# The latents' second normalization taken from the first one's scale and variance, and the order of the opening, in a two-layer cross-attention and mixture-of-experts kernel

## The chip, the cores and the metric

The kernel runs on one NeuronCore of one Trainium2 chip. The metric is the device time of one execution in microseconds (us), taken as a median over several executions: 2829.24 us for the kernel before, from three executions between 2828.84 and 2831.44. The profile is of a separate execution. Engine names are those of the profile: PE is TensorE's matrix multiplication and PEld its weight load, DVE is VectorE, ACT is ScalarE, POOL is GpSimd, SP is SyncE, which here issues most of the DMAs.

## The reference, cut to what matters

The input `x` holds 4 batches of 512 latents of 256 numbers; `ctx_1024` holds 4 batches of 1601 context rows of 256 numbers. Four layers follow one another, each added to `x`: a cross-attention with 8 heads of 128, an expert layer with two experts for each token, a second cross-attention, a second expert layer. The change touches the first cross-attention alone:

```
def _layernorm(x, axis=-1, eps=1e-05):            # outside the layer
    m, v = mean(x), var(x)
    return (x - m) / sqrt(v + eps)

def _L0_xattn_ref(x, latents, gamma_media, beta_media, gamma_lat, beta_lat, Wq, bq, Wkv, bkv, Wo, bo):
    xn = _layernorm(x, gamma_media, beta_media)         # the context
    ln = _layernorm(latents, gamma_lat, beta_lat)       # the latents
    q = ln @ Wq + bq
    kv_input = concatenate([xn, ln], axis=1)            # 1601 + 512 rows
    k, v = split(kv_input @ Wkv + bkv)
    out = softmax(q k^T / sqrt(128)) v                  # per head
    return out @ Wo + bo

x = x + _L0_xattn_ref(ctx_1024, _layernorm(x), ...)
```

The latents are normalized twice, one normalization straight after the other. The first has no gain and no shift, so its result has mean zero, and its variance follows from the variance `v` of `x`: with `s = 1/sqrt(v + eps)` it is `v * s * s`.

## The kernel before

**Stages.** The first cross-attention fills the span up to about 1575 us, the rest follows. For each of the four batches the normalized latents and context rows are turned (features on the partitions) into one tile `kvin`, which all eight heads read: the 512 latents stand in the first column group, the context rows behind them. A head takes its queries from the latents' columns of `kvin` (line 767), its keys from all columns (line 783, five pieces of which the first, `keys(0)`, covers 512 columns, the latents' among them), its values (line 817), then scores (line 834), row maximum on DVE (line 842), exponential on ACT (line 848), an exchange of blocks by DMA (line 855), a 32x32 block transpose on DVE (line 863), the weighted sum of values (line 871) and the output projection (line 882). The scores have one PSUM buffer of five banks (`a_ps_s`), so the next scores wait for the exponential of the last. All other PSUM results of this layer rotate through the two buffers of the pool `ps_t`.

**The normalization helpers.** `ln_moments` runs `bn_stats` and `bn_aggr` on DVE for each tile of 128 rows (lines 127 and 128) into `mv`, which holds mean and variance. `ln_scale` turns the variances of all tiles into scales: `ve = variance + eps` (line 137), a square root on ACT (line 144), a reciprocal on DVE (line 149) and one Newton step of four small DVE operations (lines 152 to 155). `ln_apply` subtracts the mean and multiplies by the scale (line 159), one DVE operation of 128x256 for each tile. `layernorm` is all three. A batch of latents has four tiles.

**`keys_input(b, ctx_b)`** makes the steps that fill `kvin` for one batch. `latents` normalizes `x[b]` into the tile `lat`; `latents_again` normalizes `lat` in place; `group` turns four tiles of 128 rows with PE transposes into two PSUM tiles `tp` (line 683), one for each half of the features, and writes each into `kvin` with gain and shift: the first half on DVE (line 708), the second on ACT (line 700). For batch 0, `first(n0)` takes the statistics of up to four context tiles on DVE (lines 725 and 726), their scale and a shift `away` (line 729), and applies both on ACT (line 733).

**The opening.** For batch 0 these steps are written in an order by hand, and `in_order(*computing)` keeps their instructions on PE, DVE, ACT and POOL in exactly that order (an instruction from elsewhere may stand between them):

```
latent, context = keys_input(0, ctx_b)     # latents, latents_again, group of the latents
*qk, fill = queries_keys(0)                # queries, keys(0) .. keys(4)
stats, turns = context[::2], context[1::2] # first(n0), ctx_group(n0)
for s in (latent[:2] + stats[:1] + latent[2:] + fill[:2] + stats[1:2] + turns[:1] + stats[2:3] + ...):
    s()
```

So the first context group's statistics stand ahead of the writing of the latents into `kvin`, on DVE and on ACT alike. The loads of the opening are issued by SP in an order of their own (`in_order(nc.sync)`, lines 629 to 648): `x` of batch 0, the first context group, the small vectors, the first head's parts of the weights, then the other context groups and weights.

**After the opening** the framework's scheduler sets the order on each engine from the order of the text and the dependencies; it may move an instruction ahead of others on its engine. For batches 1 to 3 the steps of `keys_input` are attached to the heads 5 to 7 of the batch before: `latents` and `latents_again` to one query tile each, `group` later. The tile `lat` has one buffer (pool `a_gone`), which between the opening and batch 1 is a scrap tile under the same tag. The Sqrt of line 144 and the Exp of line 848 need different tables on ACT; where one follows the other an `ACT_TABLE_LOAD` stands ahead of it.

Of the kernel before, what the change touches and what calls it, by code (L numbers as in the profile page):

```python
# [8 lines left out]
F32 = mybir.dt.float32  # L9
I32 = mybir.dt.int32  # L10
AF = mybir.ActivationFunctionType
ALU = mybir.AluOpType
# [4 lines left out]
P = 128  # L17
B, S, D = 4, 512, 256
M = 1601
NT = S // P  # L20
NX = B * NT
DC = D // P
EPS = 1e-5
# [51 lines left out]
def xattn_ffn_twice(ctx: ExitStack, tc: tile.TileContext, a: dict, out: bass.AP):  # L75
    nc = tc.nc
# [41 lines left out]
    def ln_moments(pool, src, n, tail=P, mv=None, some=None):  # L118

        if mv is None:  # L120
            mv = pool.tile([P, n, 2], F32, tag=f"mv{n}", name="mv")
            if tail < P:
                nc.vector.memset(mv, 1.0)
        for i in range(n) if some is None else some:
            r = rows_of(i, n, tail)
            st = pool.tile([P, 6], F32, tag="bnst", name="st")
            nc.vector.bn_stats(st[:r], src[:r, i, :])
            nc.vector.bn_aggr(mv[:r, i, :], st[:r])
        return mv

    def ln_stats(pool, src, n, tail=P):

        return ln_scale(pool, ln_moments(pool, src, n, tail), n)

    def ln_variance(pool, mv, n):
        ve = pool.tile([P, n], F32, tag=f"ve{n}", name="ve")
        nc.vector.tensor_scalar(ve, mv[:, :, 1], EPS, None, ALU.add)
        return ve

    def ln_root(pool, mv, n, ve=None):  # L140
        if ve is None:
            ve = ln_variance(pool, mv, n)
        rs = pool.tile([P, n], F32, tag=f"rs{n}", name="rs")
        nc.scalar.activation(rs, ve, AF.Sqrt)
        return ve, rs

    def ln_scale(pool, mv, n, root=None):
        ve, rs = root or ln_root(pool, mv, n)
        nc.vector.reciprocal(rs, rs)

        t = pool.tile([P, n], F32, tag=f"nt{n}", name="t")
        nc.vector.tensor_tensor(t, rs, rs, ALU.mult)
        nc.vector.tensor_tensor(t, t, ve, ALU.mult)
        nc.vector.tensor_scalar(t, t, -0.5, 1.5, ALU.mult, ALU.add)
        nc.vector.tensor_tensor(rs, rs, t, ALU.mult)
        return mv, rs

    def ln_apply(dst, src, mv, rs, i, r=P):
        nc.vector.tensor_scalar(
            dst[:r, i, :], src[:r, i, :], mv[:r, i, 0:1], rs[:r, i : i + 1], ALU.subtract, ALU.mult  # L160
        )

    def layernorm(pool, dst, src, n):
        mv, rs = ln_stats(pool, src, n)
        for i in range(n):
            ln_apply(dst, src, mv, rs, i)
# [10 lines left out]
    x = [const.tile([P, NT, D], F32, name=f"x{b}") for b in range(B)]  # L177
# [13 lines left out]
    def clear_slots(zeros, i):  # L191
# [24 lines left out]
        fill=0.0,  # L216
# [365 lines left out]
    with ExitStack() as st:  # L582

        w = st.enter_context(tc.tile_pool(name="a_w", bufs=1, side="right"))
        gone = st.enter_context(tc.tile_pool(name="a_gone", bufs=1, side="right"))
        rt = st.enter_context(tc.tile_pool(name="a_rt", bufs=1, side="right"))
        one = st.enter_context(tc.tile_pool(name="a_one", bufs=1))
        two = st.enter_context(tc.tile_pool(name="a_two", bufs=2))
# [61 lines left out]
        def add_output_bias(b):  # L650
            for i in range(NT):
                nc.gpsimd.tensor_tensor(x[b][:, i, :], x[b][:, i, :], bo, ALU.add)

        def keys_input(b, ctx_b):

            state = {}
# [5 lines left out]
                state["ctx"] = ln_scale(two, state["mv"], NM)  # L662

            def latents():
                state["lat"] = lat = gone.tile([P, NT, D], F32, tag="lat", name="lat")
                layernorm(two, lat, x[b], NT)

            def latents_again():
                layernorm(two, state["lat"], state["lat"], NT)
                if b:  # L670
                    add_output_bias(b)

# [64 lines left out]
            if b == 0:  # L737
                steps = [latents, latents_again, lambda: group(state["lat"], 0, NT, 0, gbl, P, NT)]
                return steps, [
                    f for n0 in range(0, NM, 4) for f in (lambda n0=n0: first(n0), lambda n0=n0: ctx_group(n0))  # L740
                ]
# [5 lines left out]
                lambda: moments(range(8, NM)),  # L747
                scale,
                latents,
                latents_again,  # L750
            ] + [lambda n0=n0: apply(n0) for n0 in range(0, NM, 4)]
            late = [lambda: group(state["lat"], 0, NT, 0, gbl, P, NT)]
# [157 lines left out]
        latent, context = keys_input(0, ctx_b)  # L910
        *qk, fill = queries_keys(0)

        stats, turns = context[::2], context[1::2]
        for s in (
            latent[:2] + stats[:1] + latent[2:] + fill[:2] + stats[1:2] + turns[:1] + stats[2:3]
            + turns[1:2] + fill[2:3] + stats[3:] + turns[2:3] + fill[3:4] + turns[3:] + fill[4:]
        ):
            s()
# [24 lines left out]
        for n in range(n_steps + 4):  # L943
            b, h, t = n // (H0 * NT), n // NT % H0, n % NT
# [143 lines left out]
    turns = soonst.enter_context(tc.tile_pool(name="turns", bufs=2))  # L1088
# [143 lines left out]
    with ExitStack() as st:  # L1232
        two = st.enter_context(tc.tile_pool(name="b_two", bufs=2, side="right"))
# [120 lines left out]
        again = nc.values_load(odds_i[0:1, 0:1], min_val=0, max_val=2 * E)  # L1354
# [65 lines left out]
    with ExitStack() as st:  # L1420
        one = st.enter_context(tc.tile_pool(name="c_one", bufs=1))
        two = st.enter_context(tc.tile_pool(name="c_two", bufs=2))
# [276 lines left out]
    with ExitStack() as st:  # L1699
        one = st.enter_context(tc.tile_pool(name="d_one", bufs=1))  # L1700
        two = st.enter_context(tc.tile_pool(name="d_two", bufs=2))
# [202 lines left out]
        state = {}  # L1904
# [46 lines left out]
        for k, long in enumerate(SURE):  # L1951
            i = sum(long == other for other in SURE[:k])
# [157 lines left out]
```

## Time and profile before

| | |
|---|---|
| time, median of three executions | 2829.24 us (2828.84 to 2831.44) |
| time of the profiled execution | 2828.22 us |
| its span on the core | 2826.2 us |
| mean granted TensorE clock | 0.986 |
| first scores' row maximum (line 842) starts | 51.16 us |
| first cross-attention ends, about | 1575 us |

The profiled execution's time is 2.0 us above its span, which is what lies around the span. In the rows that follow, a row of the timeline gives start, duration, engine, line, operation, output and inputs with their shapes, the number of merged instructions, and in brackets the idle time of the engine before it and what ended that idle time. A matrix product of float32 is recorded as two instructions, so `x4` for queries is two products, one for each half of the features.

### The profile page before, as it was taken

How to read it: one execution, taken by the hardware profiler on the slowest of the kernel's cores; microseconds unless marked ns; L12 is line 12 of the kernel's file. 1: busy time of each engine (PE TensorE's matmuls, PEld its weight loads, DVE VectorE, ACT ScalarE, POOL GpSimd, SP SyncE). 2: the span in 40 equal slices, each digit the busy share in tenths (PEclk: the TensorE clock that was granted, in tenths of full speed). 3: DMA queues.
4: the chain of work that ended last, by engine and by line, in shares of the span. 5: the costliest groups of instructions: out<-in, count | busy, mean ns of one | idle time of the engine just before them, and what ended most of it. 6: DMA issues, size and time to landing. Idle time of an engine off the chain costs nothing. (4 is left out here: it accounts for less than half of the span.)

```text
span 2826.2 us, 36019 instructions
## 1 busy us (share of the span) xinstructions
PE 2706.3 (96%) x13566; PEld 1851.0 (65%) x13566; DVE 1468.9 (52%) x2343; ACT 940.0 (33%) x1362; POOL 260.0 (9%) x292
## 2 busy tenths in 40 slices
PE   5999999999999999999999899998999898889998
PEld 2666666666766666766666687774455454458887
DVE  6544547544476444545444421137887878872111
ACT  3333334323233332333233211214444444442221
POOL 0000000100000000001000002001110201022542
PEclk9999999999999999999999999999999999999999
DMA  5444443433343344334334545535631111025573
GB/s 164 110 115 113 104 103 95 114 95 84 95 119 91 102 100 100 89 85 113 95 84 125 176 154 175 169 97 144 178 81 40 38 31 54 33 71 193 166 229 89
DMA packets 196435, 311.95 MB, mean 110 GB/s; under 512 B 43319, under 2 KB 117368, under 8 KB 193560
## 3 DMA queue, kind: packets, MB, share of 16 engines
q1 hardware_dynamic: 157512, 227.52, 29.4%
q0 software_dynamic: 14160, 46.31, 5.5%
q10 hardware_dynamic: 24576, 35.68, 4.9%
q8 instruction: 111, 1.82, 0.3%
q14 instruction: 76, 0.62, 0.1%
HBM read 111.73 MB, written 51.34 MB: 58 GB/s over the span
## 5 line engine op out<-in xcount | busy, mean ns | idle before, releaser
L842 DVE TENSOR_REDUCE top<-ps_s 128x1 f32<-128x2113 f32 x128 | 301.8, 2358 | 581.0 <-PE ps_s L834 581.0
L871 PE MATMUL ps_o<-pT,v 128*128 128x256 f32 x2176 | 521.6, 381 | 0.5 <-DVE inv L849 0.5
L834 PE MATMUL ps_s<-kT,qT 128*128 128x512 f32 (+1 forms) x1280 | 489.0, 526 | 5.8 <-ACT attn L848 5.8
L871 PEld LDWEIGHTS ps_o<-pT,v 128*128 128x128 f32 x2176 | 409.9, 191 | 115.1 <-issue 68.4
L848 ACT ACTIVATE attn<-ps_s,top 128x2113 f32<-128x2113 f32 x128 | 259.0, 2024 | 476.7 <-DVE top L842 452.0
L834 PEld LDWEIGHTS ps_s<-kT,qT 128*128 128x128 f32 x1280 | 241.6, 191 | 252.5 <-issue 236.6
L863 DVE STREAM_TRANSPOSE pT<-swapped 128x2176 f32<-128x2176 f32 x128 | 312.4, 2441 | 33.8 <-DMA swapped<-attn 23.7
L1195 DVE TENSOR_REDUCE tops<-ps_s 128x2 f32<-128x1024 f32 (+1 forms) x224 | 238.3, 1106 | 102.9 <-PE ps_s L1184 101.7
L783 PE MATMUL ps_k<-kvin,wkv 128*128 128x512 f32 (+1 forms) x640 | 263.6, 535 | 4.1 <-DVE mv_g L721 2.1
L1453 PE MATMUL ps_w<-asked,keyed 64*128 64x256 f32 (+1 forms) x1664 | 225.2, 405 | 35.1 <-DVE tops L1195 33.9
L817 PE MATMUL ps_v<-wkv,kvin 128*128 128x256 f32 x1088 | 254.5, 381 | 0.0
L1466 ACT ACTIVATE pT<-ps_w 128x1024 f32<-128x1024 f32 x192 | 189.8, 1022 | 150.7 <-PE ps_w L1453 139.4
L817 PEld LDWEIGHTS ps_v<-wkv,kvin 128*128 128x128 f32 x1088 | 204.8, 190 | 34.9 <-issue 4.5
L1453 PEld LDWEIGHTS ps_w<-asked,keyed 64*128 64x128 f32 (+1 forms) x1664 | 150.3, 188 | 110.2 <-DVE tops L1195 53.5
L1471 DVE TENSOR_TENSOR sum<-sum,pT 128x1024 f32<-128x1024 f32 x176 | 214.8, 1221 | 13.5 <-PE ps_o L1480 4.9
L796 ACT ACTIVATE kT<-ps_k,bqk 128x512 f32<-128x512 f32 (+1 forms) x160 | 96.9, 620 | 265.9 <-PE ps_k L783 130.5
L783 PEld LDWEIGHTS ps_k<-kvin,wkv 128*128 128x128 f32 x640 | 116.2, 192 | 78.6 <-issue 68.0
L824 ACT COPY v<-ps_v 128x512 f32<-128x512 f32 x144 | 79.9, 561 | 215.9 <-PE ps_v L817 143.9
L1184 PE MATMUL ps_s<-kv,qT 32*128 32x512 f32 (+1 forms) x1024 | 134.7, 553 | 9.3 <-DVE tops L1195 5.1
L1269 PE MATMUL ps_h<-sxT,w 128*128 128x256 f32 x512 | 116.1, 384 | 3.7 <-ACT hT L1276 3.7
L1283 PE MATMUL ps_y<-w,hT 128*128 128x256 f32 x512 | 115.1, 380 | 0.0
L1269 PEld LDWEIGHTS ps_h<-sxT,w 128*128 128x128 f32 x512 | 97.9, 192 | 20.5 <-ACT hT L1276 4.5
(302 smaller groups left out, 2525.2 us busy)
## 6 DMA issues: line engine op xcount, KB each, us to landing
swapped<-attn SPq DMA_DIRECT2D x1536, 68.0 KB, 2.0
swapped<-attn ACTq DMA_DIRECT2D x512, 68.0 KB, 2.2
w<-in_w_dram SPq DMA_DIRECT2D x32, 1024.0 KB, 6.0
rows_b<-empty SPq DMA_DIRECT2D x36, 530.0 KB, 4.4
w_e<-in_wall_dram SPq DMA_DIRECT2D x5, 2052.0 KB
cw<-in_ctxT_dram SPq DMA_DIRECT2D x4, 1601.0 KB
keyed<-kv SPq DMA_DIRECT2D x32, 200.1 KB, 3.6
ctx_b<-in_ctx_dram SPq DMA_DIRECT2D x3, 1536.0 KB
```

The source lines that it names most:

```text
L783: nc.tensor.matmul(ps[:, :n], lhsT=wkv[:, c, hs], rhs=kvin[:, c, : NB - 1, k, :] if k < 4 else kvin[:, c, NB - 1, :, :], start=c == 0, sto ...
L817: nc.tensor.matmul(ps[:, k, :], lhsT=flat_kvin[c][:, j * P : (j + 1) * P], rhs=wkv[:, c, cols], start=c == 0, stop=c == DC - 1,)
L834: nc.tensor.matmul(flat[:, j0 : j0 + n], lhsT=qT[:, t * P : (t + 1) * P], rhs=kT[:, j0 : j0 + n], start=True, stop=True,)
L842: nc.vector.tensor_reduce(top, flat[:, :L], AX.X, ALU.max, negate=True)
L848: nc.scalar.activation(attn[:, :L], flat[:, :L], AF.Exp, bias=top, accum_out=total)
L863: nc.vector.transpose(pT[:, :, k * P : (k + 1) * P].rearrange("p c (a i) -> p a c i", a=4), swapped.rearrange("p a (c i) -> p a c i", i=32),)
L871: nc.tensor.matmul(ps, lhsT=v[:, j - parts[part][0], (h % 2) * DH0 : (h % 2 + 1) * DH0], rhs=pT[:, j, :], start=j == 0, stop=j == NB - 1,)
L1195: nc.vector.tensor_reduce(tops[u][:, t : t + at // n, 2 * pair : 2 * pair + 2, j0 // 512], of, AX.X, ALU.max,)
L1269: nc.tensor.matmul(ps[:, f, :], lhsT=w1[:, c, (f0 + f) * P : (f0 + f + 1) * P], rhs=sxT[:, c, :], start=c == 0, stop=c == DC - 1,)
L1453: nc.tensor.matmul(ps[:r, s, pair * QH : (pair + 1) * QH], lhsT=keyed[o][64 * s : 64 * s + 64, pair, j * P : j * P + r], rhs=asked[u % 3][ ...
L1466: nc.scalar.activation(pT[:r], ps[:r], AF.Exp)
L1471: nc.vector.tensor_tensor(sums[u, 0], sums[u, 0], pT, ALU.add)
```

## The change

The step `latents` keeps only statistics and scale of `x[b]`. The step `latents_again` computes the second scale from the first scale and the variance, multiplies the two scales, and applies mean and product to `x[b]` at once. The opening's list of steps has the latents' `group` directly behind `latents_again`, ahead of `first(0)`.

```
             def latents():
+                state["once"] = ln_stats(two, x[b], NT)
+
+            def latents_again():
+                mv, once = state["once"]
+                ve = two.tile([P, NT], F32, tag="again", name="ve_a")
+                nc.vector.tensor_tensor(ve, once, once, ALU.mult)
+                nc.vector.tensor_tensor(ve, ve, mv[:, :, 1], ALU.mult)
+                nc.vector.tensor_scalar(ve, ve, EPS, None, ALU.add)
+                _, rs = ln_scale(two, mv, NT, ln_root(two, mv, NT, ve))
+                nc.vector.tensor_tensor(rs, rs, once, ALU.mult)
                 state["lat"] = lat = gone.tile([P, NT, D], F32, tag="lat", name="lat")
-                layernorm(two, lat, x[b], NT)
-
-            def latents_again():
-                layernorm(two, state["lat"], state["lat"], NT)
+                for i in range(NT):
+                    ln_apply(lat, x[b], mv, rs, i)
                 if b:
                     add_output_bias(b)
...
         for s in (
-            latent[:2] + stats[:1] + latent[2:] + fill[:2] + stats[1:2] + turns[:1] + stats[2:3]
+            latent + stats[:1] + fill[:2] + stats[1:2] + turns[:1] + stats[2:3]
             + turns[1:2] + fill[2:3] + stats[3:] + turns[2:3] + fill[3:4] + turns[3:] + fill[4:]
         ):
```

For a batch this takes away four `bn_stats`, four `bn_aggr`, one addition of eps and four applications on DVE, and adds four operations of 128x4 (the three that make `ve_a` and the product of the scales). The square root on ACT and the five operations behind it stay. Batches 1 to 3 run the same two steps; nothing else in the list of their steps is changed.

## The prediction, made before the changed kernel was run

> **What bounds the kernel now.** I read the engines' shares first, then busy time by stretch, then PE's waits, then the opening's timeline. The chain of waits on the page covers only the last 25 us and doesn't bear on this change.
>
> ```profile
> PE 2706.3 (96%) x13566; PEld 1851.0 (65%) x13566; DVE 1468.9 (52%) x2343; ACT 940.0 (33%) x1362; POOL 260.0 (9%) x292
> ```
> ```profile
> 24.40:50.00 25.60, 18.83 (x55) 8.70 (x55) 12.06 (x49) 11.51 (x25) 0.00 (x0) 0.87 0.37 110
> 50.00:78.40 28.40, 24.28 (x72) 12.83 (x70) 23.38 (x68) 16.61 (x20) 0.00 (x0) 0.94 0.38 96
> 78.40:1552.00 1473.60, 1473.10 (x5517) 1000.72 (x5518) 755.37 (x915) 476.32 (x655) 44.34 (x52) 1.00 0.40 101
> ```
> ```profile
> PE ps_s L834 <- ACT attn L848: 0.6, 1, 0.6
> PE ps_p L882 <- ACT oT L1013: 0.5, 1, 0.5
> ```
>
> The stretches give length, then busy time of PE, PEld, DVE, ACT and POOL, the granted clock, DMA share and GB/s. From 78.4 to 1552 us PE is busy for 1473.10 of 1473.60 us at full clock, and the last two lines are all that PE waits for there: 1.1 us. Whatever DVE or ACT does less of in that stretch is worth nothing; a time saved before 78.4 passes through whole. Before it PE is not the bound, and the change's order is made there:
>
> ```profile
> 9.18 1.38 DVE L159 TENSOR_SCALAR lat<-x,mv,rs 128x256 f32<-128x256 f32 x4
> ...
> 10.48 0.42 DVE L127 BATCH_NORM_STATS2 st<-lat 128x6 f32<-128x256 f32 x1
> ...
> 12.73 0.17 DVE L137 TENSOR_SCALAR ve<-mv 128x4 f32<-128x4 f32 x1
> ...
> 14.19 1.38 DVE L159 TENSOR_SCALAR lat<-lat,mv,rs 128x256 f32<-128x256 f32 x4
> ...
> 14.75 2.20 PE L683 MATMUL tp<-ident,lat 128*128 128x128 f32 x8 [14.75 <-DVE lat L159]
> 15.48 0.42 DVE L725 BATCH_NORM_STATS2 st<-ctx_b 128x6 f32<-128x256 f32 x1
> ...
> 19.40 0.81 DVE L708 TENSOR_SCALAR kvin<-tp,gbl 128x512 f32<-128x512 f32 x1
> 19.51 2.07 ACT L733 ACTIVATE ctx_b<-ctx_b,away,rs 128x256 f32<-128x256 f32 x4 [1.23 <-DVE away L729]
> ...
> 20.31 4.07 PE L767 MATMUL ps_q<-kvin,wq 128*128 128x512 f32 x4 [3.36 <-issue]
> 21.49 0.76 ACT L700 ACTIVATE kvin<-tp,gbl 128x512 f32<-128x512 f32 x1
> ...
> 24.41 0.75 DVE L774 TENSOR_SCALAR qT<-ps_q,bqk 128x512 f32<-128x512 f32 x1 [4.21 <-PE ps_q L767]
> ...
> 25.08 0.42 DVE L725 BATCH_NORM_STATS2 st<-ctx_b 128x6 f32<-128x256 f32 x1
> ```
>
> The transposes of the latents are done at 16.95, but DVE copies their first half out at 19.40 only, behind the first context group's statistics, and ACT the second half at 21.49, behind four context tiles. So PE stands for 3.36 us, and DVE then stands for 4.21 us for the queries (24.41) before the second context group. From 25.08 to 35.4 DVE has no gap; the opening is DVE's.
>
> **The second normalization, batch 0.** Removed between 9.18 and 12.73: four applications (9.18 to 10.48, 1.30 us) and four pairs of statistics (10.48 to 12.73, 2.25 us). The rest, from `ve` at 12.73 to the application at 14.19, stays (1.46 us, with the root on ACT and 0.27 us of waiting for it). Added are four 128x4 operations; `ve` gets in place of one of them, so three are net. Such dependent operations start 0.20 us apart (8.58, 8.78, 8.98, 9.18): 0.60 us. Net 3.55 - 0.60 = **2.95 us**: the application starts at 11.24 and ends at 12.62, PE's transposes end at 14.0.
>
> **The moved copies.** DVE now waits for the first four transposes. They follow the last application (12.62) by about 0.5 us (before, 15.57 to about 16.1), so the copy runs at 13.2 to 14.0 and DVE stands 0.6 us that it didn't. Queued behind it are the context statistics, which start at 14.0 instead of 15.48 and need 3.99 us to the end of `away` (15.48 to 19.47): 18.0. ACT copies the second half at 14.0 to 14.8, then has nothing until the context's root. PE starts the queries 0.10 us after DVE's copy (20.21 to 20.31): 14.1, finds ACT's half ready at 16.1, and ends after 4.07 us at 18.2. `qT` starts at 18.2 instead of 24.41: **6.2 us**. The two chains (context on DVE 18.0, queries on PE 18.2) end together, so what is late next is both.
>
> Does the rest follow by 6.2? On ACT the context tiles of the first group are applied at 18.05 to 20.1, only 1.5 us earlier than before, but the next in line, `kT` of `keys(0)` (26.98), would come at 20.8: 0.7 us to spare. No DMA is moved on SP. The loads: x, three context groups and tail, the small vectors and first weight parts are about 2.44 MB in one queue, and the DMA view's 2-us slices add up to 2.2 MB by 12 us and 2.87 MB by 14 us. The second group is wanted at 18.9, the third at 23.6. The gains and shifts of the latents (0.002 MB behind 1.05 MB) are in by 8, as the gain vectors behind them land 1.7 us after their issue at 6.96. I take 6.2 for everything up to 78.4.
>
> **The clock.** Queries take 4.07 us for x4 at 20.31 and 1.88 at 100.48: the array starts at half speed. The Trainium skill (TensorE: Matmul & The Clock Gate, Part 1) says that a free-running window of about 3.4 us of sustained work lifts the gate and an idle one closes it, and (Part 4) that transposes don't count as work. Moving the queries right behind the transposes then wins no speed: they take 4.07, as in my sum. If transposes did count, queries could end near 16.0 and DVE's 18.0 would decide: 6.4 us. The rule that speaks against the change is the closing: the granted clock was 0.50 from 32.8 to 39.6, and that period can fall on other work. The row bounds it: matmuls of x4 took 3.75 there against 1.95 at 41.63. One such group more or less on the path is 1.8 us either way.
>
> **Batches 1 to 3.** DVE loses per batch about 3.5 us and gains 0.8; with 755 of 1474 us busy this hides beside PE. Cover gone, it would be 8 us over three batches. PE's, POOL's and SP's order comes out the same in the built kernel. One thing moves: the root of batch 1's second scale no longer hangs on an application into `lat`, whose buffer the scrap holds, so the scheduler pulls it from about 286 us to the values of the first heads (about 82), with its table load and the reload of Exp ahead of the exponential at 87.28. ACT has 1.67 and 2.44 us idle before the copies there; the first load (1.28) and the root (0.21) fit in, the reload delays that exponential by 1.28. The Trainium skill (ScalarE: Activation LUTs, What ACT_TABLE_LOAD costs) reckons 1283 ns and a drain of 1380 ns: 2.66 us. The rows show no drain (load at 289.60, 1.28; the one at 74.93 is followed by its exponential at 76.22). Either way the next scores stand at 95.53 on PE, and the exponential ended at 89.4: room for 6 us. I put it at nothing; the same pair leaves 286 us, where it was hidden too.
>
> **The sum.** 2826.2 - 6.2 = 2820.0 span, with 2.0 around it 2822.0 for a profiled run. That run was 1.0 under the median, so 2829.24 - 6.2 = **2823.0 us**, 0.22% faster. The measurement can tell about 0.2%, 5.7 us, from no change: the forecast lies just past it.
>
> **Rivals.**
> - **Part is given back in the opening** (0.38). The half-clock period falls on `keys(0)` (its four start 0.85 us apart at half speed and 0.45 at full, which two of them had: 0.8 us), whose `kT` stands ahead of the second group's root on ACT; or on the first scores (48.22, 2.91 for x8: up to 2.9 more). Or the context chain is the true bound and only DVE's 1.5 us count (2827.7). For it: ACT's applications move by 1.5 only. Against the last: DVE's 4.21 us of standing for queries is plain in the row. Gain 1.5 to 5.6, typically 4: 2825.
> - **Slower through the clock gate** (0.07). Place: 19 to 78 us, where the second row above has 24 of 28 us busy at 0.94. Work that comes sooner leaves gaps elsewhere; if the gate closed for eight more windows of 3.4 us, each costs half its length, 1.7: 13.6 - 6.2 = 7.4 slower, 2836.6. It decides from four windows on. Against it: the order of gaps behind `qT` is the same, only earlier.
> - **The hoisted root stalls PE**: if the reload came before 78.4, where PE waits on exponentials (0.65 at 78.39), it would cost its 1.3 to 2.8: 2825. The order has it behind the copies; counted within the first rival.
>
> **Numbers.** Forecast 0.55, partial gain 0.38, slower 0.07. The range joins the forecast's own (6.2 with 1.8 on either side: 2821 to 2825) with most of the partial gain, and a little luck with the clock: 2820.0 to 2827.0. Faster by over 0.2%: 0.55; within: 0.38; slower: 0.07.
>
> **What will show it.** Line 159 on `lat` at 11.2; DVE's copy into `kvin` at 13.2; queries on PE at 14.1; `qT` at 18.2; first row maximum at 44.9 instead of 51.16; PE's waits from 72 to 1546 still about 1 us. Wrong if `qT` comes later than 19, if DVE shows a gap between 19 and 29, or if the row maximum at 84.89 - 6.2 is followed by PE waiting for `attn`.

## The result and the profile after

The changed kernel takes 2821.28 us (median of ten executions, 2819.25 to 2825.64) against 2828.28 us of the kernel before on the same chip (ten, 2824.97 to 2832.88). The ratio is 0.9976 with a 95% interval from 0.9968 to 0.9985: faster by 0.15 to 0.32%, some 7 us. The prediction said 2823.0 and 6.2. In us the interval reaches from about 4 to 9, so the times alone confirm the size only roughly; the timeline does it more closely.

The opening, from the timeline of the changed kernel (start, duration, engine, line, operation; its lines behind the change stand ten higher than before):

```profile
11.22 1.38 DVE L159 TENSOR_SCALAR lat<-x,mv,rs 128x256 f32<-128x256 f32 x4
...
11.78 2.21 PE L693 MATMUL tp<-ident,lat 128*128 128x128 f32 x8 [11.78 <-DVE lat L159]
13.17 0.81 DVE L718 TENSOR_SCALAR kvin<-tp,gbl 128x512 f32<-128x512 f32 x1 [0.57 <-PE tp L693]
13.90 0.42 DVE L735 BATCH_NORM_STATS2 st<-ctx_b 128x6 f32<-128x256 f32 x1
14.02 0.78 ACT L710 ACTIVATE kvin<-tp,gbl 128x512 f32<-128x512 f32 x1 [4.04 <-PE tp L693]
...
14.04 3.39 PE L777 MATMUL ps_q<-kvin,wq 128*128 128x512 f32 x4
...
17.59 0.16 DVE L739 SCALAR_TENSOR_TENSOR away<-mv_g,rs 128x4 f32<-128x4 f32 x1
17.68 0.75 DVE L784 TENSOR_SCALAR qT<-ps_q,bqk 128x512 f32<-128x512 f32 x1
...
28.05 3.75 PE L793 MATMUL ps_k<-kvin,wkv 128*128 128x512 f32 x4 [2.12 <-DVE mv_g L731]
...
44.40 2.36 DVE L852 TENSOR_REDUCE top<-ps_s 128x1 f32<-128x2113 f32 x1 [6.94 <-PE ps_s L844]
```

The latents are applied 2.97 us earlier than before, DVE's copy into `kvin` starts at 13.17 instead of 19.40, and `qT` at 17.68 instead of 24.41. The idle time ahead of `qT`, 4.21 us before, is gone; in its place stands 0.57 us for the transposes. The 6.7 us last: the first row maximum starts at 44.40 instead of 51.16.

Then comes the stretch in which PE is the bound, by its summary and by PE's waits:

```profile
71.70:1546.00 1474.30, 1472.98 (x5516) 1000.29 (x5517) 747.20 (x884) 475.59 (x654) 44.35 (x52) 1.00 0.40 101
```
```profile
PE ps_v L827 <- ACT v L834: 1.3, 2, 0.8
PE ps_s L844 <- ACT attn L858: 0.6, 1, 0.6
```

DVE does 8 us less here (747.20 against 755.37) and PE is busy as long as before. PE's waits, all shown above, are 1.9 us instead of 1.1.

The profiled execution is the slowest of the ten (2825.64 us), and it shows more than the opening. The first weighted sum starts 6.7 us earlier than before (79.8, before 86.5), the first weighing in the second cross-attention 7.0 us (1911.1, before 1918.1), the last one there only 2.7 us (2520.9, before 2523.6). From these two profiles alone, one would have read a gain of 2.6 us; the ten executions say 7.

### The profile page after: what moved, and what is told of

Same layout as the page of the kernel before. It is cut to its first block, busy times and chain, and to the rows that moved or that the text cites. A ratio compares the mean times of both kernels' runs of the same rounds, so it can differ in the third digit from the quotient of the medians.

```text
span 2823.9 us, 35983 instructions
## 1 busy us (share of the span) xinstructions
PE 2711.7 (96%) x13566; PEld 1853.8 (66%) x13566; DVE 1458.4 (52%) x2307; ACT 939.3 (33%) x1362; POOL 262.4 (9%) x292
```

## The experiments

The kernels were timed in groups, each beside the kernel before on the same chip. In the last group the kernel before and the changed kernel both take some 8 us longer than in the first, so ratios are compared. A ratio is not the quotient of the two medians and can differ from it by some hundredths of a per cent.

| kernel | `qT` at, us | first row maximum, us | median, us | ratio to before, 95% interval |
|---|---|---|---|---|
| before | 24.41 | 51.16 | 2828.28 | 1 |
| changed kernel | 17.68 | 44.40 | 2821.28 | 0.9976 [0.9968, 0.9985] |
| norm_only | 21.47 | 49.60 | 2825.90 | 0.9991 [0.9984, 0.9998] |
| order_only | 20.58 | 47.29 | 2825.30 | 0.9982 [0.9973, 0.9992] |
| batch0_only | 17.74 | 45.95 | 2822.30 | 0.9976 [0.9964, 0.9988] |
| later_only | 24.08 | 50.86 | 2830.84 | 1.0003 [0.9992, 1.0013] |
| after_again | 17.57 | 45.52 | 2829.60 | 0.9976 [0.9966, 0.9985] |
| warm | 17.59 | 43.09 | 2823.09 | 0.9955 [0.9942, 0.9967] |
| tail_root | 17.39 | 43.45 | 2824.91 | 0.9959 [0.9946, 0.9972] |
| warm_tail | 17.57 | 42.16 | 2823.20 | 0.9954 [0.9941, 0.9967] |

In norm_only to later_only before had a median of 2829.05, in the last four 2835.86. The arrival of `x` differs by up to 0.4 us between profiles (first statistics at 5.17 in tail_root, at 5.53 in warm), and all that follows with it.

### The normalization alone

The changed kernel with the opening's old list:

```
-            latent + stats[:1] + fill[:2] + ...
+            latent[:2] + stats[:1] + latent[2:] + fill[:2] + ...
```

> The new normalization with the opening's old list (first context statistics ahead of the latents' copies into kvin). Theory (two separate gains in the opening, then PE-bound): only the 2.95 us of DVE work are gone, everything in the opening shifts by that; qT at 21.4 instead of 24.41, first row maximum at 48.2 (before 51.16, changed kernel 44.40), time about 3 us under before. Rival (the normalization is all that counts, the order only follows it): first row maximum near 44.5, about 7 us under before. Rival (the copies' place is all): 51.2, no difference.

From its timeline:

```profile
16.45 0.81 DVE L718 TENSOR_SCALAR kvin<-tp,gbl 128x512 f32<-128x512 f32 x1
...
21.47 0.75 DVE L784 TENSOR_SCALAR qT<-ps_q,bqk 128x512 f32<-128x512 f32 x1 [4.21 <-PE ps_q L777]
...
38.65 3.32 PE L793 MATMUL ps_k<-kvin,wkv 128*128 128x512 f32 x4 [1.64 <-DVE kvin L718]
```

The whole chain stands 2.95 us earlier with the same gaps in it, to the 4.21 us of standing for the queries. The row maximum, though, came 1.56 us and not 2.95 us earlier (49.60, expected 48.2). The missing 1.4 us lie on the last row: these keys took 3.32 us, in before 1.95 us (at 41.63). The granted clock was at half from 39.1 to 42.5 here, of which more below. The ratio, 0.9991, is 0.09% of the 0.24% that the whole change brings.

### The order alone

The old two normalizations with the new list (the same edit the other way, on the kernel before).

> The old two normalizations with the new list of the opening. Theory: DVE's copy starts 3.0 us later than in the changed kernel, at 16.1, context scale done and qT at about 20.6 (before 24.41), first row maximum at 47.4, time about 3.8 us under before; together with norm_only this adds up to the changed kernel's 6.8. Rival (DVE's added wait for PE gives the gain back): qT not before 23, row maximum at 50 or later.

```profile
16.08 0.81 DVE L708 TENSOR_SCALAR kvin<-tp,gbl 128x512 f32<-128x512 f32 x1 [0.57 <-PE tp L683]
...
20.58 0.75 DVE L774 TENSOR_SCALAR qT<-ps_q,bqk 128x512 f32<-128x512 f32 x1
```

`qT` is 3.83 us earlier than before, and DVE waits 0.57 us for the transposes, as in the changed kernel. The parts add up at this point: 2.94 + 3.83 = 6.77, measured together 6.73. So the larger part of the gain at `qT` is not in the saved arithmetic but in where the copies stand. The row maximum is 3.87 us earlier (47.29, expected 47.4). In the times each part alone is faster than before; the two add up to 0.27% beside the 0.24% of the whole, and their intervals overlap, so which part is larger is read from the timeline and not from the times.

### Batch 0 alone, and batches 1 to 3 alone

batch0_only keeps the old two normalizations for `b > 0` behind an `if`, with the new list; later_only has the old ones for `b == 0` and the old list.

> New list, new normalization in batch 0, the old two normalizations in batches 1 to 3. Theory (PE hides all of batches 1 to 3): first row maximum 44.4 and a time within 1 us of the changed kernel's; PE's waits between 72 and 1546 about 1 to 2 us as in both kernels. Rival (the DVE work saved in batches 1 to 3, or the root pulled forward to the first heads, shows in the time): 2 us or more beside the changed kernel, slower if the saved work counted, faster if the pulled root cost.

> Old list and old normalizations in batch 0, the new normalization in batches 1 to 3. Theory: first row maximum at 51.2 and a time within 1 us of before; PE does not wait for the exponential that the table load delays. Rival (pulled root stalls PE in the first heads): 1.3 to 2.8 us of new PE waits between 78 and 110 and as much more time.

The ratios are 0.9976, the changed kernel's, and 1.0003. Batches 1 to 3 bring and cost nothing that can be measured; the interval of later_only alone leaves room for some 2 us gained to 4 us lost, and PE's waits narrow it. The root that the scheduler pulled forward is in later_only too, with its two table loads (ACT's timeline):

```profile
81.88 1.28 ACT L144 ACT_TABLE_LOAD   x1
83.17 0.20 ACT L144 ACTIVATE rs<-ve_a 128x4 f32<-128x4 f32 x1
...
86.93 1.28 ACT L863 ACT_TABLE_LOAD   x1
88.23 2.02 ACT L863 ACTIVATE attn<-ps_s,top 128x2113 f32<-128x2113 f32 x1
```

The first load and the root end before the next copy is due (83.52), the second delays the exponential by its 1.3 us, and PE has no new wait for `attn`: 0.6 us in total from 71.7 to 1546, as in before. PE's waits for the copies `v`, none listed in before, are 1.2 us in later_only and 1.3 us in the changed kernel, but also 1.0 in order_only, which has the old normalizations everywhere; the new arithmetic isn't needed for them.

### The changed kernel again, and PE kept at work

Two profiles had now shown a first row maximum later than their `qT` let expect. In both, norm_only and batch0_only, the granted clock fell twice in the opening. The view by stretch of batch0_only (length, then busy PE, PEld, DVE, ACT, POOL, granted clock, DMA share, GB/s):

```profile
25.10:32.00 6.90, 5.01 (x11) 2.42 (x12) 2.97 (x15) 3.48 (x9) 0.00 (x0) 0.51 0.63 182
32.00:35.30 3.30, 1.39 (x9) 0.84 (x8) 1.91 (x8) 2.06 (x5) 0.00 (x0) 1.00 0.00 0
35.30:38.70 3.40, 3.13 (x5) 0.90 (x3) 0.23 (x1) 0.45 (x2) 0.00 (x0) 0.50 0.00 0
```

The second period lies on the keys of line 798; the first row is of batch0_only, the second of the changed kernel, whose profile has one period only:

```profile
34.92 3.40 PE L798 MATMUL ps_k<-kvin,wkv 128*128 128x512 f32 x4 [1.64 <-DVE kvin L723]
```
```profile
34.88 1.95 PE L793 MATMUL ps_k<-kvin,wkv 128*128 128x512 f32 x4 [1.18 <-DVE kvin L718]
```

That is the 1.5 us between the row maxima, 45.95 and 44.40. The next run repeats the changed kernel, and "warm" adds matmuls that nobody reads:

```
+        warming = ps_o.tile([P, 2 * P], F32, tag="o", name="ps_warm")
+        def warm(n):
+            for _ in range(n):
+                nc.tensor.matmul(warming[:, :P], lhsT=ident, rhs=before, start=True, stop=True)
...
+        warm(20)
-            ... + turns[:1] + stats[2:3] + turns[1:2] + fill[2:3] + ...
+            ... + turns[:1] + [lambda: warm(4)] + stats[2:3] + turns[1:2] + [lambda: warm(8)] + fill[2:3] + ...
```

> The changed kernel once more, beside the next three. Theory: qT at 17.7 and, with one half-clock period of 6.8 us around 27 to 34, the first row maximum at 44.4; with a second period in the opening, as two other runs had, about 1.5 us later. Time about 6.8 us under before in the mean.

> The changed kernel with matmuls on PE whose result nobody reads: 20 of 128x128 ahead of the opening, 4 behind the first context group, 8 behind the second, in PE's gaps. Theory (the half-clock period lies on the path between 28 and 34, the queries' half clock does not, since qT stands behind the context scale): qT stays at 17.7, no half-clock period before 50, keys of line 793 at 28 no longer take 3.75 us, first row maximum at about 43.5 (0.9 less). Rival (the fill is in the way, or DVE alone sets the opening): 44.4 or later.

The changed kernel repeated gave the same ratio, 0.9976, and this time two separated periods of 3.4 us at half clock in the opening, with the row maximum at 45.52. In "warm" the opening's clock by stretch and PE's timeline:

```profile
14.40:17.80 3.40, 3.40 (x5) 1.33 (x4) 2.82 (x15) 0.30 (x2) 0.00 (x0) 0.50 0.93 326
20.00:27.00 7.00, 5.45 (x35) 3.87 (x35) 5.81 (x27) 3.80 (x10) 0.00 (x0) 1.00 1.08 357
27.00:34.00 7.00, 4.39 (x19) 2.25 (x18) 3.41 (x14) 5.16 (x11) 0.00 (x0) 1.00 0.37 101
```
```profile
2.12 7.31 PE L927 MATMUL ps_warm<-before,ident 128*128 128x128 f32 x40 [2.12 <-POOL before L212]
11.74 1.74 PE L693 MATMUL tp<-ident,lat 128*128 128x128 f32 x8 [2.31 <-DVE lat L159]
13.95 3.37 PE L777 MATMUL ps_q<-kvin,wq 128*128 128x512 f32 x4 [0.47 <-DVE kvin L718]
...
27.96 1.10 PE L793 MATMUL ps_k<-kvin,wkv 128*128 128x512 f32 x2 [0.33 <-DVE mv_g L731]
29.36 1.13 PE L793 MATMUL ps_k<-kvin,wkv 128*128 128x512 f32 x2 [0.30 <-ACT kvin L710]
```

From 20 to 34 the clock is full, and the keys at 28 are done by 30.5 instead of 31.8. The row maximum is 1.31 us earlier than in the changed kernel's first profile (0.9 expected) and 2.43 us earlier than in the repeated one. "No half-clock period before 50" was wrong for one: PE stood for 2.31 us at 9.4, and the clock fell at 14.4 (in warm_tail, below, too). The queries took 3.37 us in it, and `qT` stayed at 17.59: the queries' clock is not on the path here.

### The last context group's root moved forward

On ACT the root of the last context group stood behind a copy `kT` that waits for PE's keys, and DVE stood 3.99 us for it in the changed kernel, as in before. The edit moves its statistics and root ahead of those keys' copy:

```
-            + turns[1:2] + fill[2:3] + stats[3:] + turns[2:3] + ...
+            + turns[1:2] + stats[3:] + fill[2:3] + turns[2:3] + ...
```

> The changed kernel with the last context group's statistics and root written ahead of keys(1), so that on ACT the root no longer stands behind the copy kT that waits for PE. Theory: the 3.99 us that DVE stands for this root go, what is late next are PE's transposes of the third group at half clock; row maximum at 43.2 (1.2 less). Rival (PE's keys are the bound there anyway): 44.4.

> Both together. Theory: transposes of the third group end near 31.6, DVE copies them at 31.4 instead of 33.7, first row maximum at about 42.1, time about 2.3 us under the changed kernel's. Rival: no more than the better of the two.

DVE's waits between 26 and 45 us, first in the changed kernel, then in tail_root (in total, times, longest):

```profile
...
DVE rs L149 <- ACT rs L144: 4.3, 2, 4.0
DVE kvin L718 <- PE tp L693: 2.2, 1, 2.2
```
```profile
...
DVE kvin L718 <- PE tp L693: 4.0, 2, 2.6
DVE rs L149 <- ACT rs L144: 1.5, 1, 1.5
```

DVE's wait for ACT falls from 4.3 to 1.5 us, and a wait for PE's transposes, 1.8 us more, takes part of its place. The row maximum is 0.95 us earlier, of which 0.29 belong to an earlier `x` (DVE's first copy at 12.88 instead of 13.17); 0.66 remain of the 1.2 expected, as the second half of the transposes (33.52) now waits for DVE's copy. With both edits it is at 42.16, 2.24 us under the changed kernel's first profile, as expected, though the transposes of the third group did not end near 31.6: their second half, from 32.24, waits for DVE's copy here too. In the times, warm, tail_root and warm_tail have ratios of 0.9955, 0.9959 and 0.9954, each with an upper end of 0.9972 or less, against 0.9976 [0.9966, 0.9985] for the changed kernel beside them. All three beat the kernel before and stand under the changed kernel by 0.17 to 0.22%, with intervals that still overlap; which of the three is best, five executions each don't tell. These 5 to 6 us are more than the row maximum moved, 0.9 to 2.2 us against the first profile of the changed kernel and 2.1 to 3.4 us against the repeated one. A part of the rest can be seen: the first weighted sum starts at 76.9 us in warm, 78.7 in tail_root and 77.4 in warm_tail, against 80.8 in the repeated changed kernel, and warm's profile has no half-clock period between 58 and 67 us, where all the others have one. What remains is not explained.

## Why the prediction was right

**The second normalization: 2.95 us.** Predicted application at 11.24, measured 11.22, and by itself 2.94 us at `qT`. The count of instructions and the 0.20 us between dependent small operations held.

**The moved copies.** DVE's copy was put at 13.2 (13.17), the queries at 14.1 (14.04). The added wait was put at 0.6 us (0.57), with the context statistics behind it at 14.0 (13.90). "The two chains end together" was nearly so: the scale of the context was done at 17.75 and the queries at 17.43.

**What was mis-sized.** The queries were given 4.07 us, the time that they took in before; they took 3.39. At half speed throughout and with ACT's half in time they take 3.78 us, as in batch0_only; the other 0.3 us in before was standing for ACT's copy. In the changed kernel the clock also rose before they ended: the keys that follow took 1.88 us for x4, the full-speed time. (The granted clock reads 1.00 all along here, as it does over before's slow queries, so the speed at the start of an opening is read from durations.) So DVE alone set `qT`, at 17.68 and not 18.2, and the gain there was 6.7 us instead of 6.2. The prediction's other value, 6.4 with DVE deciding, used 18.0 for the context; its own chain took 3.85 us there, not 3.99. It is a near thing, and where the clock rises is luck: in batch0_only the queries ended at 17.70, just behind DVE's chain (17.64), and set `qT`.

**A step that failed: transposes as no work.** The prediction took from the Trainium skill (TensorE: Matmul & The Clock Gate, Part 4) that transposes don't count as work for the clock, so that queries right behind them win no speed. Queries of batch0_only, at half speed to their end, and of tail_root:

```profile
13.92 3.78 PE L782 MATMUL ps_q<-kvin,wq 128*128 128x512 f32 x4
```
```profile
13.74 2.65 PE L777 MATMUL ps_q<-kvin,wq 128*128 128x512 f32 x4
```

The second row speaks against that step. In tail_root the queries follow the transposes almost at once (13.69 to 13.74), and their last two start 0.43 us apart (15.37 and 15.80), which is full speed: it was reached about 1.4 us after their start. In before, where PE stood for 3.36 us between transposes and queries, PE was busy with queries and keys from 20.31 on, and the keys at 25.02 and 25.88 were still 0.86 us apart. If 1.4 us of such work in a window of 3.4 us were enough (all periods of the clock in these traces are 3.4 us or a multiple of it), the clock would have risen by 25.1 there, wherever the windows lie. So the work just ahead of the queries, the transposes with their weight loads, counted for something. How much, these profiles don't settle.

**What followed.** The shift of 6.7 us stayed whole to 44.40 and to the first weighted sum. The margin of ACT ahead of `kT` sufficed, and no load was late: the only wait for a load before 60 us is DVE's for `x`. Of the signs of being wrong, one needs a word: DVE does show a gap that begins before 29, 3.99 us from 28.66, but it is the one that begins at 35.42 in before, moved with the rest. So the prediction's "the opening is DVE's" holds up to that gap only, and tail_root gains from closing it. The cost of nothing for batches 1 to 3 fits batch0_only and later_only, and that for the pulled root is shown by PE's waits. The table load took 1.28 us and its exponential followed 1.30 us after the load's start (86.93 to 88.23), so a reload costs 1.3 us here and not the 2.66 us of the Trainium skill (ScalarE: Activation LUTs, What ACT_TABLE_LOAD costs).

**The rivals.** The partial gain through the half clock is real as a mechanism: its first place, the keys in the opening, cost 1.1 to 1.5 us in norm_only, batch0_only and the repeated run, on top of the period that all have. It comes and goes between the two profiles of the changed kernel (44.40 and 45.52), before's profile has one such period as well, and the median, 7 us faster, shows no part given back. That only DVE's 1.5 us count is refuted by order_only, which saves no arithmetic and has `qT` 3.83 us earlier. The slower rival, eight more windows at half clock before 78 us, did not occur: no profile had more than three separate periods before 78 us, and before's own has two, from 32.8 and from 66.9.

**Not forecast.** The profiled execution gave back 4.3 us in the second cross-attention (7.0 us ahead at its first weighing, 2.7 at its last). That stretch, by its summaries, of before and of the changed kernel:

```profile
1850.00:2545.00 695.00, 632.78 (x5340) 361.19 (x5339) 539.87 (x827) 302.39 (x397) 87.89 (x116) 0.97 0.27 76
```
```profile
1843.00:2542.00 699.00, 638.49 (x5332) 362.83 (x5331) 539.71 (x827) 301.69 (x396) 90.20 (x116) 0.96 0.27 76
```

DVE is busy as long as before, PE is busy 5.7 us longer with the same matmuls, and the mean clock is 0.96 instead of 0.97. This speaks for more half-clock periods in PE's gaps there, and the other profiles bear it out. From the first weighing to the last, with the time at half clock added up from the clock's periods in each trace:

| profile | first to last weighing, us | of it at half clock, us |
|---|---|---|
| before | 605.5 | 30.7 |
| batch0_only | 605.8 | 34.1 |
| later_only | 608.5 | 41.0 |
| norm_only | 609.0 | 44.2 |
| changed kernel | 609.8 | 44.4 |
| order_only | 610.7 | 47.8 |

The length goes with the time at half clock and not with the change: batch0_only has the changed opening and a short stretch, later_only the old opening and a longer one. The four profiles of the last group are longer still (612.3 to 613.0) and don't follow this order, so something else adds to them. Why a period falls where it does is not shown. The median of ten does not show such a loss.

## What to carry to other kernels

Where an order is written by hand, look first for a result that lies finished while its reader's engine serves something else: here two copies of 0.8 us, moved ahead, were worth more than eight statistics and four applications taken away. A saving counts whole only up to the place where another engine becomes the bound, so find that place in the busy time by stretch before adding anything up; 8 us less of DVE behind it were worth nothing that could be measured. In a lead-in in which TensorE has gaps, single profiles differ by more than a small change is worth: compare the point where the bound stage begins, and many executions, not the ends of two profiles.

## What the runs showed of the hardware

In all eight profiles whose gaps were left open the granted clock fell to half in the opening, before 50 us, once or twice for 3.4 or 6.8 us, at a place that differs between two executions of one kernel. With a few microseconds of matmuls without a reader in the gaps, it stayed full from 17.8 us to beyond 50 us in both profiles that had them, and `qT` stayed where it was (17.59 and 17.57, against 17.68 and 17.57 in the two profiles of the changed kernel). In both, the clock had fallen once at 14.4, behind a gap of 2.3 us on PE and the transposes (1.74 us); what of this made it fall was not tested. Queries right behind transposes reached full speed 1.4 us after their start in tail_root, queries behind 3.36 us of idle PE more than 5.5 us after theirs in before. A table load on ACT delayed the exponential behind it by its own 1.3 us. Against the kernel before, "warm" is faster by 0.33 to 0.58%; against the changed kernel the gain of 0.21% is not clear of the intervals.
